# Residual adds of a hybrid transformer block: TensorE into PSUM with a copy by ScalarE in place of VectorE's add, and a new interleaving count

## The chip, the cores and the metric

The kernel runs on one core of a Trainium2 chip. A core has a matrix engine (TensorE, PE in the profile, with its weight loads as PEld), a vector engine (VectorE, DVE), a scalar engine (ScalarE, ACT), a general engine (GpSimd, POOL) and a queue engine (SyncE, SP). Each has its own queue of instructions, taken in order; they wait for each other by semaphores. PE writes its products to PSUM; ACT and DVE read PSUM and SBUF, POOL works on SBUF. DMA engines move data between memory and SBUF, and can add while they move.

The metric is the device time of one execution in microseconds, as the median of several. Before the change: 4081.53 us, the median of 3 runs (4073.81 to 4083.79).

## What is computed

`x` has 8 sequences (batches below) of 512 tokens with 256 features, in fp32. Four residual steps follow one another, each on the layer norm of `x`:

```python
x = x + attn_a(layernorm(x))   # per token: 16 heads, 64 x 64 scores between features, causal softmax
x = x + ffn(layernorm(x))      # silu(x w1) * (x w2), gelu(h h1), gelu(h h2), h w3; hidden width 1024
x = x + attn_b(layernorm(x))   # usual causal attention over 512 tokens, 16 heads of width 16
x = x + ffn(layernorm(x))      # the same weights as above
```

Attention A is unusual. Q, K and V of a token have 16 heads of 64 numbers, and the scores are outer products, `scores[q, k] = Q[q] * K[k] / 8` for k <= q, within one token. No matmul does that: it is elementwise work over 64 x 64 / 2 numbers per token and head, and DVE, ACT and POOL share it.

## The kernel before

**Tiles.** A batch's `x` is one SBUF tile of 128 tokens x 4 token tiles x 256 features. It stays there through all four residual steps, each of which adds its result to it in place.

**Two streams.** One Python loop emits the instructions of two streams, and since the schedule is manual, the order in which they are emitted is the order on each engine's queue.

- *Stream A* (`AttentionA.step(n)`) is attention A. Its work is cut into (batch, tile i, head group g, unit u): 8 x 4 x 4 x 4 = 512 steps. Step n runs different phases of different units, as a software pipeline: project to q, k, v (PE, n + 3), copy k and q (ACT), outer products (`scores`: POOL for units 0 and 2, DVE for 1 and 3), exponentials (ACT, n - 1), times v (`weigh`: DVE, n - 2), halving by an accumulating DMA that POOL issues (`halve`), halving by POOL (`fold`), row sums (`gather`: DVE), sums into `acc` (POOL), `invert` (DVE) and `divide` (POOL, n - 5), transpose (`turn_group`: PE, n - 7), output projection (`project_out`: PE, n - 8) and, at n - 9, `add_x` on DVE.
- *Stream 2* (`after_a()`, a generator) takes a batch that has left attention A through `ffn`, `attention_b` and `ffn`. Each `yield` hands back an amount of work in units. After each of a step's three parts the loop at the end of `fast_path` draws from the generator until the amount drawn has caught up with `total` = 304.8 units per 64 steps, beginning one batch late. What is left when A's steps end is emitted alone.

So one batch of attention A runs alone first, then seven batches of A beside seven batches of stream 2, then the rest of stream 2 alone.

**The adds.** There are three places, all with a 128 x 256 fp32 tile of PSUM and one of SBUF:

- `add_x` (L881): after `project_out` (L867) of every tile and group, 128 times. The product `po` is one half of `bank`, a PSUM tile of two halves that `project`, `turn_group`, `project_out` and the transposes of the layer norm take in turn through `half_bank`. For g = 0, `bias_row` (L466) closes the sum with a product of three bf16 rows.
- `add` in `ffn` (L1133): after each tile's product with `w3`, 64 times.
- `add` in `attention_b` (L1273, inside `added`): after each tile's output projection and its bias row, 32 times.

**Deferred work.** In stream 2, `later(fn)` puts a function on a list, and `flush()` runs the list as it stood: what a function itself defers waits for the next `flush`. Both `add` functions are deferred once and call `after(i)` at once, which starts the layer norm for the next stage: `Normed.tile` emits the statistics (DVE, `moments`), and defers `scale` (POOL), `normalise` (ACT), `turn_tile` (PE), `keep` (ACT) and, for an ffn, `low` (DVE), each by one `flush` or two. The next stage begins with `nx.wait`, which flushes and yields 0.8 units until its tiles are there.

**Weights.** Weights of stream 2 come in 1 MB pieces through three buffers, `weights.ahead()` issuing the next one's DMA on POOL's or SP's queue. Stream A's come by SP.

Of the kernel before, what the change touches and what calls it, by code (L numbers as in the profile page):

```python
# [13 lines left out]
ALU = mybir.AluOpType  # L14
AX = mybir.AxisListType

P = 128
# [21 lines left out]
MC = FH // P  # L39
# [245 lines left out]
def fast_path(ctx: ExitStack, tc: tile.TileContext, k, t, flag):  # L285

    nc = tc.nc
    ident = k.ident
# [118 lines left out]
    bias16 = const.tile([P, 2, D], BF16, name="bias16")[0:3]  # L407
    ones16 = const.tile([P, P], BF16, name="ones16")
# [56 lines left out]

    def bias_row(ps, j):  # L466

        nc.tensor.matmul(ps, ones16[0:3, :], bias16[:, j, :], start=False, stop=True)

    rends = const.tile([P, 2, NB], F32, name="rends")  # L470
    means = const.tile([P, NB, 2, NT], F32, name="means")
# [10 lines left out]
    def half_bank():  # L482
        halves[0] ^= 1
        return bank[:, halves[0], :]
# [115 lines left out]
    class AttentionA:  # L600
# [33 lines left out]
        def step(self, n):  # L634

            weighed = self.at(n - 2)
            if weighed[0] is not None:
                self.weigh(*weighed)
            unit = self.at(n)
            on_pool = unit[3] in (0, 2)  # L640
            if on_pool:
                half = self.scores(*unit)
                next(half)
            if weighed[0] is not None:
                self.halve(*weighed)
            if on_pool:
                next(half, None)
            b, i, g, u = self.at(n + 40)
            if u == 0 and g == 0 and i == 0 and b > 0:
                self.x[b] = load_x(b)  # L650
            b, i, g, u = self.at(n + 10)
            if u == 0 and g == 0 and i == 0:
                self.measure(b)
            b, i, g, u = self.at(n + 8)
            if u == 0 and g == 0:
                self.live["xn"] = normed(self.x[b][:, i, :], *self.rn[b, i], "a")
            b, i, g, u = self.at(n - 5)
            if u == NU - 1:
                self.invert(b, i, g)
            b, i, g, u = self.at(n - 4)  # L660
            if u == 1:
                self.gather(b, i, g, u)
            b, i, g, u = self.at(n + 7)
            if u == 0 and g == 0:
                nc.scalar.copy(self.live[b, i], self.live.pop("ps_ln"))
            if self.at(n - 1)[0] is not None:
                self.exps(*self.at(n - 1))
            yield
            if unit[0] is not None and not on_pool:
                for _ in self.scores(*unit):  # L670
                    pass
            for args in self.sums:
                self.add_rows(*args)
            self.sums = []
            b, i, g, u = self.at(n - 5)
            if u == NU - 1:
                self.divide(b, i, g)
            b, i, g, u = self.at(n - 2)
            if u == NU - 1:
                self.small_squares(b, i, g)  # L680

            b, i, g, u = self.at(n - 4)
            if u == 0:
                self.fold(b, i, g, u)
            b, i, g, u = self.at(n - 3)
            if u == 2:
                self.fold(b, i, g, u)
            b, i, g, u = self.at(n - 9)
            if u == NU - 1:
                self.add_x(b, i, g)  # L690
            b, i, g, u = self.at(n + 2)
            if u == 0:
                self.keep_qk(b, i, g)
            b, i, g, u = self.at(n - 7)
            if u == NU - 1:
                self.turn_group(b, i, g)
            b, i, g, u = self.at(n - 8)
            if u == NU - 1:
                self.project_out(b, i, g)
            b, i, g, u = self.at(n + 3)  # L700
            if u == 0:
                self.project(b, i, g)
            yield
            b, i, g, u = self.at(n - 4)
            if u == 2:
                self.gather(b, i, g, u)
            b, i, g, u = self.at(n - 5)
            if u == 0:
                self.gather(b, i, g, u)
            b, i, g, u = self.at(n - 3)  # L710
            if u == NU - 1:
                self.gather(b, i, g, u)
            b, i, g, u = self.at(n - 7)
            if u == NU - 1:
                nc.scalar.copy(self.live["att"], self.live.pop("pta"))
            b, i, g, u = self.at(n + 8)
            if u == 0 and g == 0:
                self.live[b, i] = lnp.tile([P, DC, P], F32, tag="xnt_a", name=f"xnta_{b}_{i}", bufs=NT)
                self.live["ps_ln"] = turned_over(self.live.pop("xn"), half_bank().rearrange("p (c s) -> p c s", c=DC))
            yield  # L720
# [146 lines left out]
        def project_out(self, b, i, g):  # L867

            att, nch = self.live.pop("att"), GW // P
            po = half_bank()  # L870
            for c in range(nch):
                nc.tensor.matmul(
                    po, att[:, c, :], self.wo[b, g][:, c, :], start=(c == 0), stop=(c == nch - 1 and g > 0)
                )
            if g == 0:
                bias_row(po, 0)
            if i == NT - 1:
                self.load_wo(b + (g + 1) // NG, (g + 1) % NG)
            self.live["po"] = po

        def add_x(self, b, i, g):  # L881
            nc.vector.tensor_tensor(self.x[b][:, i, :], self.x[b][:, i, :], self.live.pop("po"), ALU.add)  # L882
            if g == NG - 1:
                self.ready.add((b, i))

# [4 lines left out]
    def later(fn):  # L890
        pending.append(fn)

    def flush():
        fns = pending[:]
        pending.clear()
        for fn in fns:
            fn()
# [111 lines left out]
    def ffn(u, b, xt, nx, after):  # L1009
# [8 lines left out]
        h = chunks(f"h0_{u}")  # L1018
# [16 lines left out]
        for m0 in range(0, MC, 2):  # L1035
# [8 lines left out]
            def products(pj, m, j, toks):  # L1044
# [10 lines left out]
            ps = [  # L1055
                [ps_f.tile([P, S], F32, tag="pf", name=f"pw{j}_{u}_{m}") for j in range(2)] for m in (m0, m0 + 1)
            ] if m0 == 0 and nx.done < NT else [None, None]
# [33 lines left out]
        for layer in range(2):  # L1091
            h_in = h
            if layer == 0:
                h = chunks(f"h1_{u}")
            else:
                h2 = [block(f"h2_{u}_{j}") for j in range(2)]
                h = lambda p, m: h2[m // 4][:, m % 4 * S :][:, :S]
            for m0 in range(0, MC, 2):
# [14 lines left out]
                for n, step in enumerate(steps):  # L1113
                    for j, p, c in step:
# [4 lines left out]
                            start=(p == 0 and c == 0),  # L1119
                            stop=(p == 1 and c == MC - 1),  # L1120
# [9 lines left out]
            flush()  # L1130
            yield 1.8

        def add(i, po):  # L1133
            nc.vector.tensor_tensor(xt[:, i, :], xt[:, i, :], po, ALU.add)
            after(i)

        w3 = weights.take().rearrange("p (c f) -> p c f", c=MC)
        for i in range(NT):
            po = ps_f.tile([P, D], F32, tag="pf", name=f"pof_{u}_{i}")
            for c in range(MC):  # L1140
                nc.tensor.matmul(  # L1141
                    po, h(0, c)[:, i * P : (i + 1) * P], w3[:, c, :], start=(c == 0), stop=(c == MC - 1)
                )
            flush()
            if i == 1:
                weights.ahead()
            later(lambda i=i, po=po: add(i, po))
            yield 3.6
        flush()

    def attention_b(b, xt, nx, after):
# [115 lines left out]
        def added(i, yt):  # L1267
            po = ps_f.tile([P, D], F32, tag="pf", name=f"pob_{b}_{i}")
            for c in range(DC):
                nc.tensor.matmul(po, yt[:, c, :], wvp[:, 1, c, :], start=(c == 0), stop=False)  # L1270
            bias_row(po, 1)

            def add():  # L1273
                nc.vector.tensor_tensor(xt[:, i, :], xt[:, i, :], po, ALU.add)
                after(i)

            later(add)

        ys, yts2 = {}, {}
        for n in range(NT + 2):  # L1280
# [19 lines left out]
    def after_a():  # L1300

        nonlocal weights
        weights = Weights()
        nx = {}

        def tile(u, b, part, i):
            if i == 0:
                nx[u] = Normed(u, b, a.x[b], part)
                nx[u].whole = u[:2] == "1_"
            nx[u].tile(i)  # L1310

        def head(b, i):

            if b < NB:
                assert (b, i) in a.ready
                tile(f"1_{b}", b, "f", i)

        for i in range(NT):
            head(0, i)
        for b in range(NB):  # L1320
            xt = a.x[b]
            yield from ffn(f"1_{b}", b, xt, nx.pop(f"1_{b}"), lambda i: tile(f"b{b}", b, "b", i))
            yield from attention_b(b, xt, nx.pop(f"b{b}"), lambda i: tile(f"2_{b}", b, "f", i))
            yield from ffn(f"2_{b}", b, xt, nx.pop(f"2_{b}"), lambda i: head(b + 1, i))
            for i in range(NT):
                nc.sync.dma_start(t.out[b, i * P : (i + 1) * P, :], xt[:, i, :])

# [1 line left out]


    each = NT * NG * NU
    total = 304.8
    ET = mybir.EngineType
    with tc.manual_schedule(engines={ET.PE, ET.DVE, ET.Activation, ET.Pool}):
        a = AttentionA()
# [101 lines left out]
```

## Time and profile before

| | |
|---|---|
| median of 3 runs | 4081.53 us (4073.81 to 4083.79) |
| the profiled execution | 4079.68 us |
| its span, first to last instruction | 4077.9 us |
| instructions | 36814 |
| granted clock of TensorE, mean | 0.829 |
| share of the DMA engines by GpSimd's queue / SP's queue | 61.7% / 6.8% |

The profile is of that one execution. A row of a group of instructions reads: line, engine, operation, output <- inputs with their shapes, xcount | busy us, mean ns of one | idle time of the engine just before them, and who ended most of it. A digit in the row of slices is the engine's busy share in tenths, in one fortieth of the span (102 us). A row of waits gives the waiting instruction, the one waited for, the total in us, the count and the longest. PE's products of fp32 tiles are counted as two instructions each, and each has a weight load of its own.

The largest groups of each engine:

| engine | line and what it does | count | busy us |
|---|---|---|---|
| PE | L1115 products of the hidden layers | 4096 | 1056.6 |
| DVE | L804 `weigh`, units 0 to 2 | 768 | 899.6 |
| DVE | L841 row sums of w | 384 | 601.9 |
| POOL | L780 outer products | 512 | 1075.2 |
| POOL | L815 `fold` | 256 | 639.6 |
| ACT | L794 exponentials, units 0 to 2 | 384 | 734.2 |

The chain of waits (the work that ended last, followed back) is by engine: DVE 23%, POOL 13%, PE 11%, DMA 8%, ACT 6%, time in which no wait shows 5%.

### The profile page before, as it was taken

The numbers are of one execution on the slowest core, as the hardware profiler recorded it, in microseconds if no ns is written. First come the engines' busy times: TensorE is split into PE (matmuls) and PEld (weight loads), VectorE is DVE, ScalarE is ACT, GpSimd is POOL, SyncE is SP. The second block draws the span as 40 slices with busy tenths as digits, with TensorE's granted clock in tenths as the row PEclk, the third lists the DMA queues.
The fourth block names the chain that finished last, engine by engine and source line by source line (L and its number), as shares of the span: only waits on it lengthen the run. The fifth ranks groups of instructions, "written<-read, shape, count | busy, mean of one in ns | idle before, by whom it ended". The sixth has DMA issues, their size and how long they took to land.

```text
span 4077.9 us, 36814 instructions
## 1 busy us (share of the span) xinstructions
PE 2879.3 (71%) x11880; PEld 1948.2 (48%) x11880; DVE 3456.9 (85%) x4001; ACT 2284.2 (56%) x2927; POOL 3095.8 (76%) x3051
## 2 busy tenths in 40 slices
PE   1533377677876877758776787768876678767988
PEld 0311155255643655346553565436653556436847
DVE  4899988998999888889889898998889989896115
ACT  2333365666755765556655666557655567555342
POOL 6788887887888887788888787888887878786211
PEclk6555578788987988879888898879888788878999
DMA  8576777767866777658777687768776687766304
GB/s 247 104 147 142 144 183 174 150 163 190 209 154 123 193 178 193 149 130 207 176 180 144 160 201 201 155 135 205 167 188 147 146 199 183 164 135 179 136 26 171
DMA packets 118650, 671.01 MB, mean 165 GB/s; under 512 B 12704, under 2 KB 31915, under 8 KB 43824
## 3 DMA queue, kind: packets, MB, share of 16 engines
q0 software_dynamic: 78336, 570.46, 61.7%
q1 hardware_dynamic: 40112, 98.11, 6.8%
q8 instruction: 96, 1.57, 0.2%
q14 instruction: 106, 0.87, 0.1%
HBM read 255.90 MB, written 9.96 MB: 65 GB/s over the span
## 4 chain that ended last, share of the span: by engine, by line
DVE 23%; POOL 13%; PE 11%; DMA 8%; ACT 6%; issue 5%; POOLq 0%; ACTq 0%; DVEq 0%
DVE red L841 9%; DMA w<-w 8%; DVE w L804 6%; PE ph L1115 4%; POOL w L780 4%; ACT w L794 2%; POOL w L815 2%; POOL acc L848 2%; DVE ws L804 2%; DVE ws L780 2%; PE pqkb L1161 2%; PE pof L1141 2%; PE pw L1047 1%; POOL h L1031 1%; DVE w L780 1%
## 5 line engine op out<-in xcount | busy, mean ns | idle before, releaser
L1115 PE MATMUL ph<-h,hidden 128*128 128x512 f32 x4096 | 1056.6, 415 | 69.9 <-POOL h L1031 43.1
L780 POOL TENSOR_TENSOR w<-k 128x1024 f32<-128x1024 f32 x512 | 1075.2, 2100 | 12.5 <-ACT k L758 8.7
L794 ACT ACTIVATE w<-w 128x2048 f32<-128x2048 f32 x384 | 734.2, 1912 | 618.2 <-POOL w L780 405.7
L1115 PEld LDWEIGHTS ph<-h,hidden 128*128 128x128 f32 x4096 | 800.9, 198 | 278.2 <-POOL h L1031 53.3
L804 DVE TENSOR_TENSOR w<-w,qv 128x1024 f32<-128x1024 f32 x768 | 899.6, 1213 | 34.4 <-ACT w L794 34.4
L841 DVE TENSOR_REDUCE red<-w 128x128 f32<-128x1024 f32 (+1 forms) x384 | 601.9, 1568 | 124.4 <-DMA w<-w 79.2
L815 POOL TENSOR_TENSOR w<-w 128x1024 f32<-128x1024 f32 x256 | 639.6, 2499 | 50.7 <-DMA w<-w 50.5
L810 POOL DMA_DIRECT2D w<-w x384 | 337.5, 879 | 397.3 <-issue 157.4
L848 POOL TENSOR_TENSOR acc<-acc,red 128x256 f32<-128x256 f32 (+1 forms) x640 | 471.7, 737 | 178.8 <-DVE red L841 157.6
L841 DVE TENSOR_REDUCE red<-ws 128x256 f32<-128x2048 f32 (+1 forms) x256 | 435.5, 1743 | 0.0
L804 DVE TENSOR_TENSOR ws<-ws,qv 128x1024 f32<-128x1024 f32 (+3 forms) x512 | 299.0, 646 | 43.4 <-ACT ws L794 43.3
L742 PE MATMUL qv<-wqv,xnta 128*128 128x512 f32 x512 | 305.0, 727 | 42.2 <-DVE ws L804 38.2
L1047 PE MATMUL pw<-xnt,gate 128*128 128x512 f32 (+2 forms) x1152 | 300.4, 418 | 43.6 <-ACT silu L1023 18.0
L794 ACT ACTIVATE ws<-ws 128x1920 f32<-128x1920 f32 x128 | 231.3, 1807 | 143.5 <-DVE ws L780 143.0
L737 PE MATMUL bank<-wk,xnta 128*128 128x256 f32 x512 | 178.0, 481 | 184.6 <-DVE x L882 177.8
L780 DVE TENSOR_TENSOR w<-qv,k 128x1024 f32<-128x1024 f32 x256 | 301.2, 1218 | 3.6
L780 DVE TENSOR_TENSOR ws<-qv,k 128x1024 f32<-128x1024 f32 (+3 forms) x512 | 299.9, 648 | 0.0
L864 PE MATMUL bank<-ident,acc 128*128 128x128 f32 x256 | 65.8, 348 | 324.4 <-ACT k L757 312.2
L1047 PEld LDWEIGHTS pw<-xnt,gate 128*128 128x128 f32 x1152 | 226.8, 212 | 104.5 <-ACT silu L1023 27.1
L1080 ACT ACTIVATE h<-ph,s_sb 128x512 fp32r<-128x512 f32 (+1 forms) x256 | 170.8, 688 | 175.0 <-PE ph L1115 173.4
L1223 ACT ACTIVATE eb<-psb 128x256 f32<-128x256 f32 (+3 forms) x512 | 182.1, 443 | 139.8 <-PE psb L1220 139.4
L1141 PE MATMUL pof<-w,h 128*128 128x256 f32 x1024 | 245.1, 399 | 21.3 <-ACT h L1080 21.3
(137 smaller groups left out, 4558.5 us busy)
## 6 DMA issues: line engine op xcount, KB each, us to landing
w<-w POOLq DMA_DIRECT2D x384, 1024.0 KB, 7.7
hidden<-in_h POOLq DMA_DIRECT2D x128, 1024.0 KB, 7.9
gate<-in_w12p POOLq DMA_DIRECT2D x32, 1024.0 KB, 8.5
w<-w_d SPq DMA_DIRECT2D x16, 1024.0 KB
wqv<-wqv_d SPq DMA_DIRECT2D x31, 512.0 KB
wo<-in_wo SPq DMA_DIRECT2D x32, 256.0 KB, 6.7
wbqk<-wbqk_d SPq DMA_DIRECT2D x8, 1024.0 KB
w<-in_h SPq DMA_DIRECT2D x8, 1024.0 KB, 7.3
```

The costliest lines, as they stand in the source:

```text
L742: nc.tensor.matmul(qv.rearrange("p j f -> p (j f)"), xnt[:, c, :], wqv[:, c, :], start=(c == 0), stop=(c == DC - 1),)
L780: eng.tensor_tensor(e, rows(q).to_broadcast(shape), columns(kt[:, 0]).to_broadcast(shape), ALU.mult)
L794: nc.scalar.activation(e, e, AF.Exp, scale=C**-0.5)
L804: nc.vector.tensor_tensor(ev, e, columns(qv[:, 1]).to_broadcast(list(e.shape)), ALU.mult)
L810: nc.gpsimd.dma_start(w[:, :2048], w[:, 2048:], accum_op=ALU.add)
L815: nc.gpsimd.tensor_tensor(w[:, :1024], w[:, :1024], w[:, 1024:2048], ALU.add)
L841: nc.vector.tensor_reduce(red, self.columns_of(w, n, off, nsq), AX.X, ALU.add)
L848: nc.gpsimd.tensor_tensor(rows, rows, part.rearrange("p a (x i) -> p a x i", i=n), ALU.add)
L1047: nc.tensor.matmul(pj[:, toks], w[:, m % 4, j, c, :], xs[:, p, c, toks], start=(p == 0 and c == 0), stop=(p == 1 and c == DC - 1),)
L1115: nc.tensor.matmul(pss[j], w[:, j, c, :], h_in(p, c), start=(p == 0 and c == 0), stop=(p == 1 and c == MC - 1),)
L1141: nc.tensor.matmul(po, h(0, c)[:, i * P : (i + 1) * P], w3[:, c, :], start=(c == 0), stop=(c == MC - 1))
L1223: nc.scalar.activation(es[h], scs[h], AF.Exp)
```

## The change

The three adds become products on PE: after the last product of a sum, `plus` adds `ident` (the 128 x 128 identity, fp32) times the tile of `x`, so that `x + result` stands in PSUM, and ACT copies it over `x`. `bias_row` no longer closes the sum; `plus` does. In stream 2 the copy is deferred as the add was, and `after(i)` is now deferred by one `flush` more. Since an `after` can thus run when the next stage has begun, the records of normalised tiles are read instead of taken out, and the batch number is bound in the lambdas. `total` goes from 304.8 to 309.5.

```diff
     def bias_row(ps, j):
 
-        nc.tensor.matmul(ps, ones16[0:3, :], bias16[:, j, :], start=False, stop=True)
+        nc.tensor.matmul(ps, ones16[0:3, :], bias16[:, j, :], start=False, stop=False)
+
+    def plus(ps, xi):
+
+        nc.tensor.matmul(ps, ident, xi, start=False, stop=True)
...
             if u == NU - 1:
-                self.add_x(b, i, g)
+                self.new_x(b, i, g)
...
-                    po, att[:, c, :], self.wo[b, g][:, c, :], start=(c == 0), stop=(c == nch - 1 and g > 0)
+                    po, att[:, c, :], self.wo[b, g][:, c, :], start=(c == 0), stop=False
                 )
             if g == 0:
                 bias_row(po, 0)
+            plus(po, self.x[b][:, i, :])
...
-        def add_x(self, b, i, g):
-            nc.vector.tensor_tensor(self.x[b][:, i, :], self.x[b][:, i, :], self.live.pop("po"), ALU.add)
+        def new_x(self, b, i, g):
+            nc.scalar.copy(self.x[b][:, i, :], self.live.pop("po"))
...
-        def add(i, po):
-            nc.vector.tensor_tensor(xt[:, i, :], xt[:, i, :], po, ALU.add)
-            after(i)
+        def new_x(i, po):
+            nc.scalar.copy(xt[:, i, :], po)
+            later(lambda: after(i))
...
-                    po, h(0, c)[:, i * P : (i + 1) * P], w3[:, c, :], start=(c == 0), stop=(c == MC - 1)
+                    po, h(0, c)[:, i * P : (i + 1) * P], w3[:, c, :], start=(c == 0), stop=False
                 )
+            plus(po, xt[:, i, :])
             flush()
...
-            later(lambda i=i, po=po: add(i, po))
+            later(lambda i=i, po=po: new_x(i, po))
...
             bias_row(po, 1)
-
-            def add():
-                nc.vector.tensor_tensor(xt[:, i, :], xt[:, i, :], po, ALU.add)
-                after(i)
-
-            later(add)
+            plus(po, xt[:, i, :])
+
+            def new_x():
+                nc.scalar.copy(xt[:, i, :], po)
+                later(lambda: after(i))
+
+            later(new_x)
...
-            yield from ffn(f"1_{b}", b, xt, nx.pop(f"1_{b}"), lambda i: tile(f"b{b}", b, "b", i))
-            yield from attention_b(b, xt, nx.pop(f"b{b}"), lambda i: tile(f"2_{b}", b, "f", i))
-            yield from ffn(f"2_{b}", b, xt, nx.pop(f"2_{b}"), lambda i: head(b + 1, i))
+            yield from ffn(f"1_{b}", b, xt, nx[f"1_{b}"], lambda i, b=b: tile(f"b{b}", b, "b", i))
+            yield from attention_b(b, xt, nx[f"b{b}"], lambda i, b=b: tile(f"2_{b}", b, "f", i))
+            yield from ffn(f"2_{b}", b, xt, nx[f"2_{b}"], lambda i, b=b: head(b + 1, i))
...
-    total = 304.8
+    total = 309.5
```

## The prediction

> **What bounds the kernel now.** I read the profile in this order: busy shares and slices, busy time by stretch, groups by shape, VectorE's waits, the order in time around one add, and the chain at the end.
>
> ```profile
> PE 2879.3 (71%) x11880; PEld 1948.2 (48%) x11880; DVE 3456.9 (85%) x4001; ACT 2284.2 (56%) x2927; POOL 3095.8 (76%) x3051
> ...
> DVE  4899988998999888889889898998889989896115
> ```
>
> VectorE (DVE) is the busiest engine, and the last three slices are different: there it nearly idles. So there are stages. Busy time by stretch (us, then busy time of PE, PEld, DVE, ACT, POOL, the granted clock, DMA):
>
> ```profile
> 400.00:500.00 100.00, 33.63 (x64) 17.04 (x64) 99.86 (x107) 37.98 (x40) 85.25 (x75) 0.57 0.67 140
> ...
> 1912.00:2379.00 467.00, 349.13 (x1463) 235.34 (x1462) 424.52 (x497) 288.72 (x369) 383.03 (x377) 0.86 0.73 170
> ...
> 3740.00:4078.00 338.00, 310.17 (x1497) 232.56 (x1495) 99.75 (x136) 110.36 (x211) 58.62 (x96) 0.98 0.35 123
> ```
>
> Three regimes. **Attention A alone** (to 504 us): DVE is full; from one `add_x` to the next, that is for one (tile, group) of four steps, 24.1 us pass. **Both streams** (504 to about 3740): the adds of 112 groups lie between 503.8 and 3767.8 us, so 29.1 us a group; DVE is busy 424.5 of 467 us (91%), PE 75% at a clock of 0.86, ACT 62%, POOL 82%. **Tail** (the last batch's second stream, 338 us): PE is busy 92% and is the bound. DVE's idle 9% in the middle is not free time for anything; its waits between 504 and 3740 us are these (total, times, longest):
>
> ```profile
> DVE red L841 <- DMA w<-w: 72.0, 28, 8.0
> DVE silu L1026 <- ACT silu L1023: 66.4, 34, 5.0
> DVE xnt L978 <- ACT xnt L971: 44.0, 21, 7.6
> DVE red L841 <- POOL w L815: 40.7, 25, 5.8
> DVE w L804 <- ACT w L794: 29.3, 15, 6.5
> ```
>
> They are scattered head-of-line waits; no single engine paces the middle but DVE itself.
>
> **What is removed from DVE.** 224 adds: 128 in `add_x`, 64 in `ffn`, 32 in `attention_b`.
>
> ```profile
> L882 DVE TENSOR_TENSOR x<-x,bank 128x256 f32<-128x256 f32 x128 | 47.4, 371 | 11.9 <-PE bank L872 11.9
> ...
> L1134 DVE TENSOR_TENSOR x<-x,pof 128x256 f32<-128x256 f32 x64 | 26.2, 410 | 89.6 <-PE pof L1141 89.3
> ...
> L1274 DVE TENSOR_TENSOR x<-x,pob 128x256 f32<-128x256 f32 x32 | 13.0, 407 | 1.5 <-PE pob L468 1.1 <-ACT xn L534 0.4
> ```
>
> A row's mean overstates what vanishes, because neighbours overlap. The order in time shows it:
>
> ```profile
> 2040.19 0.37 DVE L882 TENSOR_TENSOR x<-x,bank 128x256 f32<-128x256 f32 x1
> 2040.47 2.34 DVE L804 TENSOR_TENSOR ws<-ws,qv 128x1024 f32<-128x1024 f32 x4
> ```
>
> The next instruction starts 0.28 us after the add does, and 0.28 is the median over all 128. The stream's adds are followed by the statistics of the same data and hold the queue 0.34 to 0.45 us; I take 0.40. [...] by the spacing 128 x 0.28 + 96 x 0.40 = 74 us. The trace decides.
>
> In the A-alone stage all of it counts: 16 groups x 0.28 = **-4.5 us**. In the middle a group loses 0.28 + 12 x 0.40 / 16 = 0.58 us of DVE work (a batch's 16 groups carry 12 tile adds of the stream). How much of that reaches the time is where I choose. If the idle share stayed 9%, 0.64 us; if half were eaten by waits that don't shrink (a DMA landing or a POOL sum is not faster because DVE comes sooner), 0.29. DMA and POOL waits are 113 of about 300 us of DVE's idle time, the rest are waits for ACT; I take 0.50, near the upper end: 112 x 0.50 = **-56 us**.
>
> **What is added to PE.** 224 products of `ident` with a 128x256 fp32 tile; each fp32 product is two instructions in this profile.
>
> ```profile
> L872 PE MATMUL bank<-wo,att 128*128 128x256 f32 x512 | 173.8, 472 | 17.9 <-ACT att L715 17.8
> ...
> 3784.10 13.83 PE pof L1141 x64
> ```
>
> The last line is from the chain's end: 64 such instructions in 13.83 us, 0.216 us each at full clock, so 0.43 us a product. In the middle that is 1.75 products a group, 0.9 us at the clock of 0.86, on an engine with 7 us free per group; POOL and DMA don't see it. DVE's waits for PE are 1.3 us in total there, so I cost it at nothing; if that cover went, 0.9 x 112 = 100 us. In the tail PE is the bound: 12 products x 0.43 = **+5.2 us**.
>
> **What is added to ACT.** 224 copies PSUM to SBUF, like `att<-bank` (L715, mean 377 ns; spacing 0.25 to 0.40 us). ACT gains about 0.5 us on 18 us per 29 us group. The changed program's order of functions on ACT has 317 changes of table against 323, so 6 loads of 1.28 us go. The copy of `new_x` stands behind the exponentials of `ws` (L794) and ahead of those of `acc` and of the next unit, which `weigh` on DVE and, through it, the DMA of `halve` wait for. [...] If the copy had to wait for PE, the exponentials would wait too, and each us of waiting would cost up to a us of the group. The trace: in every second group PE had finished with the bank over 6.5 us before the exponentials of `ws` ended (under 3.0 us in a tenth of the groups; DVE waited there once, 11.9 us, at the end of A). With 0.43 us more on PE the copy does not wait. [...] by the rows it is zero; I take zero. The copy even starts some 2 us before the add did (ACT's exponentials end a median 2.3 us before it), so PE gets `bank` back sooner: its waits on L882 were 42.6 us between 600 and 3740 us. PE isn't the bound there; I cost this at nothing.
>
> **The order.** `after` (moments, scales, the next stage's normalised tile) now runs one `flush` later, on DVE behind ACT's copy. No DMA is moved by it: the loads of weights stay at their places on SP's and POOL's queues, and the stores of `out` on SP wait for ACT's write in place of DVE's. In the middle other work lies beside it. In the tail the last tile of three stages pays the hop: a copy of 0.37 in place of an add of 0.41, and one more crossing; my estimate is 0.3 to 0.5 us each, **+1.3 us**.
>
> **The count.** Adding what `after_a` yields in one batch gives 307.2 units, and 309.6 after the change (three more waits of 0.8). The loop hands out `total` per batch, 304.8 before: over the seven batches beside A the second stream falls 7 x 2.4 = 16.8 behind, and 323.4 units are left when A's steps end. With 309.5 against 309.6, 308.8 are left: one batch and no more. What leaves the tail is the third projection of batch 6, which stands on the chain as the 13.83 us above. Counted from where A stops pacing (11 steps before the end, 375 units in some 343 us, 0.915 us a unit; each step now hands out 0.07 more, 14.6 - 0.9 = 13.3 units less): 13.3 x 0.915 = **-12.2 us**. These units run beside A instead and bring DVE 13.3 x 0.14 us (the stream's 43 us of DVE a batch over 307): **+1.9 us**.
>
> **Sum** against the profiled execution, 4079.68 us (its span 4077.9 and 1.8 around it): -4.5 - 56 + 5.2 + 1.3 - 12.2 + 1.9 = -64.3, so 4015.4. The median of the runs, 4081.53, is 1.85 higher; carried over: **4017 us**.
>
> **Rivals.**
> 1. *The waits eat it.* In the middle DVE gets ahead and then stands before a DMA sum or a POOL sum that comes when it came. For it: 113 us of its waits are of that kind. Against it: POOL (82%) and DMA wait for DVE's results in turn (`POOL acc L848 <- DVE red L841`, 157.6 us in all). A group gains 0.1 us: -4.5 - 11 - 3.8, 4062.
> 2. *More than DVE's own time.* Earlier banks let PE run ahead, and the 66.4 us of waits for `silu` shrink by a third. 0.75 us a group: -84 in place of -56, 3989.
> 3. *Slower: PE and ACT in line.* In the middle PE waits for A's `k` and for `xn`, then ACT for PE, then DVE for ACT: if this chain, not DVE, sets the group, 0.9 us of PE and 0.3 of ACT are added to it, 112 x 1.2 = +134 us on the forecast: 4151. It decides once PE's end comes over 6.5 us later than now. DVE's 91% speaks against it.
> 4. *The count does nothing.* The shifted 13 units cost beside A what they save: 4029; it lies in the forecast's range.
>
> **Chances.** Forecast with rival 4 0.63, rival 1 0.19, rival 2 0.11, rival 3 0.07. The forecast's own range: 0.29 to 0.64 us a group, 4001 to 4041. Down to 3988 it takes in rival 2; up to 4060 most of rival 1. A change under 0.3% (12 us) can't be told from none. Rival 1 ends within it a quarter of the time: faster 0.88, same 0.05, slower 0.07.
>
> **What would show it.** DVE's busy time should fall by 70 to 80 us, with 224 instructions fewer, PE gain 448 and ACT about 218. The A-alone group should be 23.8 us, the middle group 28.6. The stretch after A's last group should start with the last batch's own LayerNorm, not with L1141 of batch 6, and be about 6 us shorter in all. No exponential of ACT should wait behind a copy that waits for PE. Wrong it would be if the middle group stays at 29 us with DVE at 89%, or if ACT's waits for the projected bank appear.

## The result, and the profile after

The changed kernel takes 4011.74 us, the median of its runs, against 4082.66 us for the kernel before: a ratio of 0.9827 with a 95% interval from 0.9805 to 0.9849, so 1.7% faster, about 71 us. One of its four executions took 4794.92 us at a granted clock of 0.56, the other three 4009.55 to 4012.9 us at 0.84 to 0.85; the ratio leaves that one out. The forecast was 4017. The total is right by luck, and most of its reasons are not: the experiments show that nearly all of the gain comes from the one number in the last line of the diff, and next to none of it from the adds. Two errors of some 50 us each, of opposite sign, cancel in the sum.

First the page of the changed kernel: busy times, then VectorE's busy tenths.

```profile
PE 2958.0 (74%) x12328; PEld 2012.2 (50%) x12328; DVE 3376.7 (84%) x3777; ACT 2337.2 (58%) x3145; POOL 3098.1 (77%) x3051
...
DVE  4899988998889888998989988998889988897115
```

DVE has 224 instructions and 80.2 us less to do, PE 448 instructions more, ACT 218 more. The span fell from 4077.9 to 4007.6 us. By stretch: attention A alone, one batch of the middle (the same one as before), and the stretch behind A's last `new_x`:

```profile
400.00:500.00 100.00, 40.57 (x74) 19.62 (x75) 99.86 (x104) 41.53 (x46) 87.85 (x78) 0.62 0.70 144
1886.60:2346.10 459.50, 360.33 (x1536) 247.75 (x1535) 414.49 (x467) 297.98 (x400) 382.44 (x377) 0.88 0.74 175
3707.60:4007.60 300.00, 274.44 (x1337) 202.85 (x1335) 82.46 (x104) 104.90 (x210) 49.47 (x82) 0.98 0.31 108
```

A group of the A-alone stage takes 23.7 us (24.1 before). The middle, from the last copy of batch 0 (498.6 us) to that of batch 7 (3707.6), takes 3209 us against 3264: 28.7 us a group against 29.1. The last stretch takes 300.0 us against 310.1. The first two are what the forecast asked for, and the third is 10 us shorter where 6 were forecast; still they don't say why. DVE's waits in the middle already look odd for a kernel that VectorE is said to pace (waiting instruction, the one waited for, total us, times, longest):

```profile
DVE red L845 <- DMA w<-w: 87.3, 38, 4.9
DVE red L845 <- POOL w L819: 76.5, 29, 5.6
DVE silu L1031 <- ACT silu L1028: 52.4, 24, 5.0
DVE xnt L983 <- ACT xnt L976: 28.8, 22, 3.4
DVE ws L808 <- ACT ws L798: 24.4, 15, 2.4
DVE w L808 <- ACT w L798: 17.2, 14, 3.6
```

The waits for sums (L845, L841 before) rose from 113 to 164 us, as rival 1 had it. The longest wait for `xnt` fell from 7.6 to 3.4 us, which removing adds doesn't explain.

### The profile page after: what moved, and what is told of

It is laid out like the page before. It is cut to its first block, busy times and chain, and to the rows that moved or that the text cites. A ratio compares the mean times of both kernels' runs of the same rounds, so it can differ in the third digit from the quotient of the medians.

```text
span 4007.6 us, 37678 instructions
## 1 busy us (share of the span) xinstructions
PE 2958.0 (74%) x12328; PEld 2012.2 (50%) x12328; DVE 3376.7 (84%) x3777; ACT 2337.2 (58%) x3145; POOL 3098.1 (77%) x3051
## 4 chain that ended last, share of the span: by engine, by line
DVE 38%; PE 16%; POOL 14%; DMA 12%; issue 8%; ACT 8%; POOLq 0%; DVEq 0%; ACTq 0%
DVE red L845 15%; DMA w<-w 12%; DVE w L808 10%; PE ph L1120 5%; ACT w L798 3%; POOL w L819 3%; DVE ws L808 3%; POOL w L784 3%; PE pqkb L1167 3%; DVE ws L784 3%; POOL acc L852 3%; DVE w L784 2%; POOL w L814 2%; DVE acc L856 2%; POOL h L1036 2%
## 5 line engine op out<-in xcount | busy, mean ns | idle before, releaser
L845 DVE TENSOR_REDUCE red<-w 128x128 f32<-128x1024 f32 (+1 forms) x384 | 601.8, 1567 | 171.6 <-DMA w<-w 94.6
L845 DVE TENSOR_REDUCE red<-ws 128x256 f32<-128x2048 f32 (+1 forms) x256 | 435.5, 1743 | 0.0
L784 DVE TENSOR_TENSOR w<-qv,k 128x1024 f32<-128x1024 f32 x256 | 301.3, 1219 | 3.6
L856 DVE RECIPROCAL acc<-acc 128x256 f32<-128x256 f32 x128 | 223.2, 1744 | 12.3 <-POOL acc L852 12.3
```

What stands on the lines that cost most here:

```text
L784: eng.tensor_tensor(e, rows(q).to_broadcast(shape), columns(kt[:, 0]).to_broadcast(shape), ALU.mult)
L845: nc.vector.tensor_reduce(red, self.columns_of(w, n, off, nsq), AX.X, ALU.add)
L856: nc.vector.reciprocal(acc[:, 0, :], acc[:, 0, :])
```

## The experiments

Ratios are to the kernel before, run in between on the same chip, with the 95% interval; a difference in us is the difference of ratios times the median of before in that comparison.

**1. The parts, one at a time.** `count_only` changes one number of the kernel before; `adds_only` takes that number back in the changed kernel (as far as needed to fall behind by 2.4 units a batch, as before).

```diff
 count_only, on the kernel before
-    total = 304.8
+    total = 307.1
 adds_only, on the changed kernel
-    total = 309.5
+    total = 307.2
```

> The kernel before with total = 307.1 in place of 304.8 (it yields 307.2 a batch), adds as they were. Forecast's term: 14.6 fewer units in the tail, -12.2 +1.9 = -10 us. From the trace of after, where 72 products of a hidden layer (16.4 us) no longer stand behind the last add of A: up to -15 us. Rival 'the count does nothing': 0.

> The changed kernel with total = 307.2 in place of 309.5, so that stream 2 falls behind by 2.4 units a batch as before (324.0 units are left at the end of A, 323.4 before). Forecast's terms without the count: -4.5 -56 +5.2 +1.3 = -54 us. If the count is the larger part of the gain: -35 or less. If the count does nothing: -71, the whole of it.

`adds_A` and `adds_2` make the change for one stream's adds alone.

```diff
 adds_A, on the kernel before (bias_row with stop=False for stream A)
+            plus(po, self.x[b][:, i, :])
...
-            nc.vector.tensor_tensor(self.x[b][:, i, :], self.x[b][:, i, :], self.live.pop("po"), ALU.add)
+            nc.scalar.copy(self.x[b][:, i, :], self.live.pop("po"))
 adds_2, on the changed kernel (add_x and its sum as before)
-            plus(po, self.x[b][:, i, :])
...
-            nc.scalar.copy(self.x[b][:, i, :], self.live.pop("po"))
+            nc.vector.tensor_tensor(self.x[b][:, i, :], self.x[b][:, i, :], self.live.pop("po"), ALU.add)
...
-    total = 309.5
+    total = 307.2
```

> Only the 128 adds of stream A by PE and ACT; stream 2 and total as before. DVE sets the pace and gives back 86% of 0.28 us a group: -4.5 -27 = -31 us; A-alone group 23.8 us. Rival 'PE and ACT in line' or 'the waits eat it': -15 us or less, all of it in the A-alone stage and little in the middle. Rival 'more than DVE's own time' (earlier bank): -40 us or more.

> Only the 96 adds of stream 2 by PE and ACT, with after one flush later, total = 307.2 so that it falls behind as before. 84 in the middle x 0.40 us x 86% = -29, the tail +6.5: -22 us; A-alone group 24.1 us as before. Rival 'the waits eat it': 0 to +6 us.

| kernel | median us | ratio | against before | expected |
|---|---|---|---|---|
| count_only | 4010.67 | 0.9837 [0.9824, 0.9849] | -66 us | -10 to -15 |
| adds_only | 4066.11 | 0.9970 [0.9958, 0.9982] | -12 us | -54 |
| adds_A | 4073.02 | 0.9990 [0.9983, 0.9997] | -4 us | -31 |
| adds_2 | 4070.23 | 0.9978 [0.9969, 0.9987] | -9 us | -22 |

The count alone gives what the whole change gives. The adds give 12 us without it; on top of it nothing that shows: the changed kernel, run once more beside the last experiments (`after_2`), has 0.9835 [0.9820, 0.9850], count_only 0.9837.

Where count_only gains is read from the times at which `invert` starts for a batch's last group, batch by batch from 1 to 7 (us a batch, worked out from the traces):

| | | sum |
|---|---|---|
| before | 460.0 467.6 478.6 468.5 460.4 469.8 465.8 | 3270.7 |
| count_only | 455.9 462.5 456.9 461.6 462.1 464.2 453.4 | 3216.6 |
| changed | 456.4 461.9 461.0 461.0 456.7 463.5 452.4 | 3212.9 |
| adds_only | 459.5 468.9 465.2 465.9 458.1 465.4 467.0 | 3250.0 |

54 us are gained in the middle, with the very instructions of the kernel before but for two of ACT's table loads (321 against 323, 1.28 us each; phase2 below has 317 and is slower than count_only). Nor is it the granted clock: count_only's executions had 0.835 to 0.837, those of `adds_A` 0.831 to 0.843, and they took 4073.02. Behind the last add of A it took 298.1 us (4006.5 - 3708.4) against 310.1: 12.0 us. That second part is the forecast's term within 0.2 us; the first wasn't in it at all.

**2. Is it the place, or the falling behind?** With 304.8 units handed out against 307.2 needed, stream 2 stands half a step later against A's steps in each batch. `phase1` and `phase2` keep the right count but start stream 2 one or two steps later, so that it stands nearly still at another place (307.1 against 307.2 units still adds 0.1 a batch).

```diff
 phase1, on count_only (phase2: 13)
-                while 3 * spent * each < total * (3 * (n - each - 11) + part + 1):
+                while 3 * spent * each < total * (3 * (n - each - 12) + part + 1):
```

> The kernel of count_only (adds on VectorE, total = 307.1), with stream 2 started one step later, so that it stands at the same place against A's steps in every batch, but 4.8 units further back. Phase theory (it is the place of stream 2 against A that costs, and the kernel before drifted through bad places): at 4.8 to 7.2 units of lag the kernel before took 478.6 and 468.5 us a batch, so about 473 in place of 459: +90 to +105 us against count_only, about 4105. Drift theory (only the falling behind costs, a fixed place costs nothing but the 3.6 units that the tail grows): 4014.

> As phase1, started two steps later (9.6 units). Phase theory: at 9.6 to 12 units of lag the kernel before took 460.4 us a batch, so near count_only's 459: +10 to +40 us against it, 4020 to 4050, and less than phase1. Drift theory: +7 us for the 7.2 units in the tail, 4017, a little more than phase1.

phase1 took 4072.04 us, 0.9971 [0.9960, 0.9982]; phase2 4044.29 us, 0.9909 [0.9893, 0.9924]. Against count_only that is +55 and +29 us, of which the longer stretch behind A's last add takes 3 and 9 (301.3 and 307.2 us against 298.1). The drift theory falls: a nearly fixed place can cost as much as a wandering one. A batch takes 459.5 us on the mean at the first place, 467.3 at the second, 463.5 at the third. The order is what the place theory asked for, but the size for phase1 is little more than half: the single batches of before, from which it was taken, owe part of their 478.6 to something else, and at phase1's fixed place the batches still range from 460.2 to 475.9 us.

What a place can do is seen in the order of time. Here is the kernel before in batch 4, where one group took 37.4 us (start, duration, engine, line, what; in brackets the idle time before it and who ended it):

```profile
1941.57 0.18 DVE L521 BATCH_NORM_AGGREGATE mv<-st 128x2 f32<-128x6 f32 x1
...
1942.81 1.00 POOL L856 TENSOR_TENSOR acc<-acc 128x256 f32<-128x256 f32 x1
1943.50 2.61 POOL L815 TENSOR_TENSOR w<-w 128x1024 f32<-128x1024 f32 x1
...
1946.20 0.21 POOL L525 TENSOR_SCALAR rstd<-mv 128x1 f32<-128x1 f32 x1
...
1947.69 0.60 ACT L534 ACTIVATE xn<-x,shift,rstd 128x256 f32<-128x256 f32 x1 [8.47 <-POOL shift L528]
...
1948.34 0.69 PE L544 MATMUL ps_ln<-ident,xn 128*128 128x128 f32 x2 [8.64 <-ACT xn L534]
1948.58 0.42 DVE L978 TENSOR_TENSOR xnt<-ps_ln,xnt 128x256 fp32r<-128x256 f32 x1 [2.07 <-ACT xnt L971]
...
1952.21 0.42 DVE L978 TENSOR_TENSOR xnt<-ps_ln,xnt 128x256 fp32r<-128x256 f32 x1 [3.21 <-ACT xnt L971]
```

Stream 2's layer norm has its statistics at 1941.75. Its next step, four small instructions on POOL, stands behind A's `divide` and `fold` and starts at 1946.20. ACT and PE stand for over 8 us until it comes through, and VectorE, whose next instruction in line is the norm's `xnt`, waits 2.07 and later 3.21 us, with A's next products (L780, at 1952.55) behind it in its queue. At another place another of A's instructions stands in front. In count_only's batch 4 the same group took 34.2 us. In the same stretch of all runs (504 to 3700 us) VectorE waits for `xnt` on ACT 44.0 us before, 17.5 in count_only, 41.6 in phase1, 30.3 in phase2. All its waits for ACT together are 176 us before and 109 in count_only (163 and 161 in phase1 and phase2). Its waits for sums rose meanwhile, from 113 to 136 us, so that all its waits fell from 294 to 252. VectorE's rows in count_only, to be held against those of before:

```profile
DVE red L841 <- DMA w<-w: 68.3, 33, 4.3
DVE red L841 <- POOL w L815: 67.4, 27, 4.6
DVE silu L1026 <- ACT silu L1023: 54.2, 23, 5.0
DVE xnt L978 <- ACT xnt L971: 17.5, 21, 3.4
DVE ws L804 <- ACT ws L794: 14.1, 12, 1.6
DVE h L1086 <- ACT ph L1082: 12.4, 18, 2.5
DVE w L804 <- ACT w L794: 10.5, 12, 1.7
```

phase1 shows one such meeting switching. Its last bit of drift makes a few instructions change places on the queues between batches 4 and 5. In the eighth group of the batch (from `invert` to `invert`) A's `divide` and `fold` (L856, L815) stand behind stream 2's norm (from L525) on POOL in batch 4, and ahead of it in batch 5:

```profile
2084.47 0.21 POOL L525 TENSOR_SCALAR rstd<-mv 128x1 f32<-128x1 f32 x1
...
2087.42 0.72 POOL L856 TENSOR_TENSOR acc<-acc 128x256 f32<-128x256 f32 x1
2088.11 2.35 POOL L815 TENSOR_TENSOR w<-w 128x1024 f32<-128x1024 f32 x1
...
2550.93 1.00 POOL L856 TENSOR_TENSOR acc<-acc 128x256 f32<-128x256 f32 x1
2551.62 2.61 POOL L815 TENSOR_TENSOR w<-w 128x1024 f32<-128x1024 f32 x1
2554.32 0.21 POOL L525 TENSOR_SCALAR rstd<-mv 128x1 f32<-128x1 f32 x1
```

With the norm in front the group takes 30.2 to 31.5 us (batches 1 to 4), with `divide` and `fold` in front 36.0 to 37.4 (batches 5 to 7). In batch 3 of the kernel before, where they stand in front in the same way, it takes 37.5. That is some 6 of the 16 us between phase1's batches 4 and 5; what each of the moved instructions costs isn't separated, and the order of these three alone doesn't decide: in batch 6 of before the two stand in front of a norm as well, and the group takes 27.0.

**3. What is VectorE's time worth, and what do PE and ACT charge?** `no_add_A_c` is count_only without stream A's adds and with nothing in their place (so attention A's result is missing from x). `adds_A_c` is count_only with A's adds on PE and ACT, that is adds_A with `total = 307.1`. The two doses repeat work of the changed kernel.

```diff
 no_add_A_c, on count_only
-            nc.vector.tensor_tensor(self.x[b][:, i, :], self.x[b][:, i, :], self.live.pop("po"), ALU.add)
+            self.live.pop("po")
 pe_dose, on the changed kernel (none is a tile of zeros)
+            for _ in range(2):
+                nc.tensor.matmul(po, ident, none, start=False, stop=False)
             plus(po, self.x[b][:, i, :])
 act_dose, on the changed kernel
-            nc.scalar.copy(self.x[b][:, i, :], self.live.pop("po"))
+            po = self.live.pop("po")
+            for _ in range(3):
+                nc.scalar.copy(self.x[b][:, i, :], po)
```

> count_only with the 128 adds of stream A left out and nothing in their place (attention A's result is not added to x). VectorE theory (it sets the pace in the middle, the forecast's 86%): -31 us against count_only, 3980. Waits theory (VectorE sets the pace only in the 24.1 us groups, about 5 of 16 in a batch, and the others wait for ACT, POOL or DMA): 16 + 7 x 5 groups x 0.28 = -14 us, and up to a third of the rest, -21 at most.

> The right count (total = 307.1) with only the 128 adds of stream A by PE and ACT, stream 2's adds on VectorE: the part of the change that should pay, without the tail's price. Waits theory (A's adds pay in the A-alone stage and in the groups that VectorE fills, and PE and ACT do them for nothing): like no_add_A_c, 0.980 of before, 10 us below the changed kernel. If PE and ACT charge for them in the middle: no better than the changed kernel, 0.983 or above.

> The changed kernel with two more products of the same shape (identity times a tile of zeros) ahead of plus in each of stream A's 128 sums: the outputs stay the same, PE gets 0.86 us at full clock, about 1.0 us in the middle, more per group. Forecast (PE's products are hidden in the middle): 0 to +10 us. Rival 'PE and ACT in line': up to 112 x 1.0 = +112 us.

> The changed kernel with stream A's copy done three times over in place of once: ScalarE gets 0.5 to 0.7 us more per group, ahead of the exponentials of the next unit. Forecast (ACT's copies are hidden): 0 to +10 us. Rival 'PE and ACT in line': up to 112 x 0.6 = +67 us.

> The changed kernel once more, beside the three below on the same chip, as the base that they are held against: 0.983 of the kernel before.

| kernel | median us | ratio | held against | difference |
|---|---|---|---|---|
| no_add_A_c | 3998.59 | 0.9795 [0.9781, 0.9808] | count_only | -17 us |
| adds_A_c | 4005.66 | 0.9822 [0.9808, 0.9835] | count_only | -6 us |
| after_2 | 4012.26 | 0.9835 [0.9820, 0.9850] | count_only | -1 us |
| pe_dose | 4035.66 | 0.9894 [0.9878, 0.9909] | after_2 | +24 us |
| act_dose | 4015.43 | 0.9845 [0.9832, 0.9858] | after_2 | +4 us |

Such a difference is good to some 8 us. Taking 36 us of VectorE's time away for nothing (128 x 0.28) gave 17, give or take 8: the waits theory's number, and about half of the forecast's 31. The traced executions of no_add_A_c and count_only took 4002.99 and 4008.24 us, only 5 apart; the 17 comes from the ratios over all executions. The products on PE are not free: 256 more of them cost 24 us, 0.09 us each; by that price, if one product costs what each of two more does, the 128 of the change give back 12 of the 17. PE is idle for over a fifth of the middle (busy 360.33 of 459.50 us in the changed kernel's row), and still they count. The copies on ACT cost nothing that shows. -17 + 12 = -5 agrees with the -6 of adds_A_c, within the error of either.

Of the 24 us of pe_dose some 16 can be followed through stream 2's layer norm: ACT's waits for the norm's transposes on PE (`ps_ln`) and VectorE's waits for ACT's copy of them both grow by 16 us (after_2 first, then pe_dose, 504 to 3700 us):

```profile
DVE xnt L983 <- ACT xnt L976: 28.8, 22, 3.4
ACT xnt L976 <- PE ps_ln L548: 18.2, 13, 2.6
...
DVE xnt L988 <- ACT xnt L981: 45.2, 20, 3.5
ACT xnt L981 <- PE ps_ln L551: 34.2, 13, 4.3
```

Why removing VectorE's work pays only about half, the groups show. These are single groups of count_only's batch 4 (from one `invert` to the next; columns as above, DMA's busy share last but one):

```profile
1915.69:1949.87 34.18, 27.92 (x103) 20.75 (x101) 29.38 (x35) 28.04 (x33) 30.98 (x27) 0.87 0.66 156
...
2004.19:2035.73 31.54, 26.35 (x109) 20.54 (x108) 24.20 (x27) 20.08 (x21) 21.64 (x19) 0.97 0.92 257
...
2141.17:2165.23 24.06, 16.82 (x95) 6.99 (x96) 24.03 (x27) 14.59 (x27) 20.87 (x19) 0.82 0.65 131
...
2190.52:2223.40 32.88, 18.33 (x58) 12.27 (x58) 32.33 (x57) 14.51 (x20) 27.75 (x38) 0.60 0.49 96
```

The mean of 29 us a group is a mean of unlike things. While `attention_b` runs its exponentials (third line), a group takes 24.06 us as in the A-alone stage and VectorE fills it; so does it where a layer norm brings it much work (fourth, 32.33 of 32.88). In the ffn groups (first and second) VectorE is busy 24 to 29 of 31 to 34 us, and other things end them: in the first POOL and ACT have 31 and 28 us of work, in the second VectorE waits for an accumulating DMA and POOL's sum behind it while the DMA engines are 92% busy. Whether the weights' loads slow that DMA there was not shown. In the changed kernel the third kind of group became 23.7 us, and the others stayed about as they were: 31.77 in place of 31.54 for the second.

**4. The tail.** `tail_dve` is the changed kernel with the old adds in the last batch's stream 2 (and no `plus` there).

```diff
         def new_x(i, po):
-            nc.scalar.copy(xt[:, i, :], po)
-            later(lambda: after(i))
+            if alone:
+                nc.vector.tensor_tensor(xt[:, i, :], xt[:, i, :], po, ALU.add)
+                after(i)
+            else:
+                nc.scalar.copy(xt[:, i, :], po)
+                later(lambda: after(i))
```

> The changed kernel with the old adds (VectorE, after called at once) in stream 2 of the last batch alone, which is the tail. Forecast's price of the change in the tail, 12 products of 0.43 us and three hops of 0.4: -6.5 us against the changed kernel, 4005. If PE's products are hidden in the tail: 0.

4007.66 us, 0.9815 [0.9801, 0.9828]; by ratio 5 us below the changed kernel's first comparison and 8 below after_2's, with intervals that overlap. The stretch behind the last `new_x` is 296.4 us (4012.8 - 3716.4) against 300.0 and, in after_2, 302.3. By these stretches the price is 4 to 6 us. Two other pairs of traces with nearly the same amount left for the tail give 6 (adds_only, 316.1 against 310.1 before) and 9 (adds_2, 319.1); by the medians it isn't clear of the noise.

adds_A_c and tail_dve are the fastest kernels that compute everything, 4 to 7 us ahead of the changed one by the medians; the intervals don't part them from it, nor from count_only.

## Why the prediction was right, and where it was not

**The total**: forecast 4017, measured 4012. It came from two wrong terms of opposite sign, and that they cancel is luck.

**The middle: wrong.** The step is "They are scattered head-of-line waits; no single engine paces the middle but DVE itself", and on it "112 x 0.50 = -56 us". The 91% was a mean over groups that VectorE fills and groups that it doesn't. Leaving 31 us of A's adds out of the middle, at no price, paid some 13 by the ratios (17 less the A-alone stage's 4). With the right count, the whole change shortened the middle by 4 us (3216.6 to 3212.9). Rival 1, "the waits eat it", held for the adds: with the right count the waits for sums rose from 136 us (count_only) to 164 as the adds left VectorE. The other 23 of the rise from 113 came with the count.

**The count: its tail right, its main effect not seen.** The forecast had -12.2 us for what leaves the tail (14.6 - 0.9 units are 13.7, not its 13.3, which would make it -12.5), and count_only measured -12.0. But "+1.9" for the middle was -54: I took the number for an amount of work to be shifted, and not for the place at which two streams meet in in-order queues. The prediction's own traces held a hint that I didn't follow: batches of one and the same work between 460.0 and 478.6 us. Rival 4, "the count does nothing", was the wrong way round (its 4029 should be 4027.5 by the forecast's own terms).

**PE: priced at nothing, costs some 12 us by the dose.** The step "DVE's waits for PE are 1.3 us in total there, so I cost it at nothing" looked at direct waits alone. In the changed kernel's middle nothing of VectorE's waits for PE directly, but what it waits for on ACT waits for PE, as pe_dose's rows show. The bound given for the lost cover, 0.9 us a group, was far too high: by the dose 1.75 products cost 0.16.

**ACT: right for stream A, not quite for stream 2.** Two copies waited for PE in stream A, 5.1 us in all, and three copies in place of one cost 4 us or nothing. These are the copies of the changed kernel (busy us, mean ns, then the idle time of ACT before them and who ended it):

```profile
L887 ACT COPY x<-bank 128x256 f32<-128x256 f32 x128 | 46.4, 362 | 5.1 <-PE bank L472 5.1
...
L1139 ACT COPY x<-pof 128x256 f32<-128x256 f32 x64 | 23.5, 368 | 42.2 <-PE pof L472 42.2
...
L1281 ACT COPY x<-pob 128x256 f32<-128x256 f32 x32 | 11.8, 367 | 21.5 <-PE pob L472 21.5
```

The 42.2 us are all but 0.7 in the tail. Of the 21.5 us 16.3 lie in the middle, where one copy a batch waits 2.3 us; the next on ACT's queue is then another copy of stream 2 (L1270) and no exponential. So what the forecast weighed, exponentials held up behind a copy that waits for PE, cost little, as its rows had it.

**A alone and the tail: right.** 23.7 us a group where 23.8 was forecast. The tail's price of +6.5 was 4 to 9, by single traces.

**What should have shown it.** The busy times came as forecast (-80.2 on DVE, where the spacing gave 74). But the signs chosen couldn't tell the theories apart: a middle group of 28.6 us was to speak for VectorE's pace, was measured at 28.7, and had another cause. One sign failed outright and was a warning: behind A's last copy the changed kernel still starts with the third projection of batch 6, not with the last batch's layer norm.

```profile
3686.02 14.54 PE ph L1120 x64
3700.78 5.47 PE ph L1120 x24
3707.54 3.45 PE pof L1146 x16
```

A's last copy stands three steps, some 14 units, ahead of the loop's end; what left the stretch behind it was the 16.4 us of hidden products that stood there before.

**Open:** what most of the meetings of the two streams cost at which place: one of some 6 us is shown above, and the norm's waits are about half of the 54 us. Places between whole steps weren't tried.

## What to carry to other kernels

Where two hand-interleaved streams share in-order queues, the place at which they meet can be worth as much as the work itself: here half a step of drift a batch cost 1.6% (54 us in the middle and 12 of work left over at the end), more than removing 80 us of work from the busiest engine gained. Before a mean busy share is used to price removed work, cut the stage into its periods: where the periods differ, as here, the work can be worth its time in those alone that this engine fills (taking 36 us away paid 17). And when one change has a part that "only puts a number right", run that part alone first.

## What was not expected of the hardware

PE was idle over a fifth of the middle, and still 256 more products, a pair of them 1.03 us at the median in pe_dose's trace, cost 24 us (pe_dose against after_2). And the fp32 add of 128x256 with one operand in PSUM, 0.37 us by its record in the forecast's lines, was followed on VectorE by the next instruction after 0.28 us (the median of the 128 in stream A, all followed by work on other tiles); where the statistics of the same data came next, it was after 0.42 (L1134, the median of 60) and 0.45 us (L1274, of 32), all in the kernel before. ACT's copy of the same tile, 0.35 us, was followed after 0.26 here, and after 0.24 to 0.26 in the 13 such pairs of the changed kernel with no wait between:

```profile
2040.93 0.35 ACT L887 COPY x<-bank 128x256 f32<-128x256 f32 x1
2041.19 0.38 ACT L1139 COPY x<-pof 128x256 f32<-128x256 f32 x1
```
